# Bulk loads beside the steps of an attention kernel: two parts of 512 KB in a step instead of three of 256 KB

## The chip, the cores and the metric

The kernel runs on one core of one Trainium2 chip. Its time is the device time of one execution in microseconds (us), as the median of several runs; less is better. A profile of one execution gives the rows that are quoted here. In it PE is TensorE, DVE is VectorE, ACT is ScalarE, POOL is GpSimd and SP is SyncE, which does nothing here but issue transfers. A name with q (ACTq, SPq) is the engine's instruction queue while it issues a transfer.

## The reference

Four layers follow one another on `x` of 4 images x 512 channels x 32x32, all in float32, each as x + layer(group_norm(x)). The change touches only the first, an attention over T = 1024 tokens whose 8 heads are mixed before the softmax:

```python
q = einsum('oc,bct->bot', w_q, xf).reshape(b, heads, hd, t)     # k and v likewise
attn = einsum('bhdq,bhdT->bhqT', q, k) * hd ** -0.5
attn = einsum('gh,bhqT->bgqT', w_head, attn)                    # the head mix
attn = softmax(attn, axis=-1)
attn = (attn - mean) / sqrt(var + EPS) * in_gamma + in_beta     # mean, var over queries and keys of a head
out  = einsum('bhqT,bhdT->bhqd', attn, v)
out  = out.reshape(b, t, c) @ w_proj.T + b_proj                 # then back to channels, added to x
```

Behind it come a gate per channel from a small simulated quantum circuit (layer 1), an ordinary attention of 8 heads (layer 2) and a lookup of the 8 best rows out of 2048 in a memory (layer 3).

## The kernel before

Layer 0 takes the images one after another, and each image in 32 steps of 32 query rows. What is made of an image in its steps runs on for some steps into those of the next one, so that the projections of the last image and the preparation of the next lie beside the steps of the present one.

A step, in the order in which the engines get its work:

- PE makes the scores of the first half of the keys into the PSUM tile `sc` (L423), and ACT copies them to `ss` (L429).
- Then comes whatever was planned for the beginning of the step; the bulk loads are there. They are issued on ACT's queue by `beside` (L249).
- PE mixes the heads of an earlier step (`mix`, L443) from the tile `s2`, ACT takes the exponential of the two halves (`exps`, L450), DVE turns the result (`turn_keys`, L456).
- PE makes the scores of the other half of the keys, and ACT copies them to `ss` as well.
- Eight transfers of 128 KB from `ss` to `s2`, the relay (L436, `s<-ss` in the profile), bring the 8 heads of a query together on the partitions, as the mix needs them. Four are issued by SP and four by POOL, in turn.

The relay of step s is read by the mix of two steps later. `ss` and `s2` have two buffers each, so the first copy to `ss` in step s + 2 also waits for the relay of step s to have read it. Each engine keeps the order in which its work is written (`pin`).

Besides, SP issues stores of pieces (`o<-o` L562, `x<-xr` L626), and POOL transfers for the row sums (L515, L523).

The bulk loads are two generators, advanced once in a step, and each advance issues the next group:

- `next_image(b, ...)`: the next image `xn` (2 MB) and the weight `w_q` (1 MB; after the last image the operand of layer 2, `Wq`), in steps 28 to 31 of each image.
- `collect(b, last)`: the attention's output `of` of the image before (2 MB, back from DRAM) and the projection weight `w_p` (1 MB), in steps 7 to 10 of images 1 to 3. The last image's is loaded in another way (`last`), which the change doesn't touch.

Both use `in_threes`: a list of twelve loads of 256 KB, 128 rows of 2 KB each, three in a step over four steps. Steps 28 and 29 load six parts of `xn`, step 30 the last two and a part of `w_q`, step 31 the three others; in `collect` likewise, where the tile for `w_p` is taken in step 9.

After the steps, the weight is used by `take_q` and by `put_quarter`, and `xn` is normalised in place (L357) as the image's statistics are there.

Of the kernel before, what the change touches and what calls it, by code (L numbers as in the profile page):

```python
# [19 lines left out]
T = 1024  # L20
KC = C // P
TC = T // P
NB = 512
# [18 lines left out]
def fast_net(ctx: ExitStack, tc: tile.TileContext, a: dict, out: bass.AP, flag: bass.AP):  # L42
# [43 lines left out]
    for i in range(P // NH):  # L86
        nc.scalar.dma_start(
            out=whp[i * NH:(i + 1) * NH], in_=a["w_head"].rearrange("r m g -> (r m) g")
# [13 lines left out]
        out=gavg_v, in_=gavg_v, compare_op=ALU.is_ge, fill=0.0, base=0,  # L102
# [3 lines left out]
        out=gavg_v, in_=gavg_v, compare_op=ALU.is_ge, fill=0.0, base=GSZ - 1,  # L106
# [99 lines left out]
    o_rows = [dram.tile([P, TC, NB], F32, tag=f"o_{b}", name=f"o_{b}") for b in range(B)]  # L206
# [22 lines left out]
    def big(tag, name):  # L229

        return apool.tile([P, KC, T], F32, tag=tag, name=name)
# [3 lines left out]
    def eight_k(shape, name, at=None):  # L235

        if at is None:
            at = turns8[0] % 3
            turns8[0] += 1
        return apool.tile(shape, F32, tag=f"w{at}", name=name)  # L240
# [6 lines left out]
    def beside(out, in_):  # L247

        pin(nc.scalar.dma_start(out=out, in_=in_))  # L249

    def in_threes(loads):

        for i in range(0, len(loads), 3):
            for out, in_ in loads[i:i + 3]:
                beside(out, in_)
            yield

    def next_image(b, key, src):

        I = img[b]  # L260
        xn = I["xn"] = big("xn", f"xn_{key}{b}")
        w = I[key] = eight_k([P, KC, C], f"{key}_{b}", 2)
        return in_threes([
            (xn[:, k, n * NB:(n + 1) * NB], src[:, k, n * NB:(n + 1) * NB])
            for k in range(KC) for n in range(T // NB)
        ] + [(w[:, k], a[key][:, k]) for k in range(KC)])

    def run_out(gen):
        for _ in gen:
# [296 lines left out]
    def collect(b, last):  # L566


        I = img[b]
        if last:  # L570
            I["of"] = o_full
            nc.sync.dma_start(out=wp_full, in_=a["w_proj"])
            nc.sync.dma_start(out=I["of"].rearrange("p (j x) -> p j x", j=TC), in_=o_rows[b])
            return
        I["of"] = big("xn", f"of_{b}").rearrange("p k t -> p (k t)")
        of = I["of"].rearrange("p (j x) -> p j x", j=TC)
        yield from in_threes([(of[:, j], o_rows[b][:, j]) for j in range(6)])
        w = I["w_p"] = eight_k([P, KC, C], f"w_p_{b}", 2)
        yield from in_threes([(of[:, j], o_rows[b][:, j]) for j in range(6, TC)] + [
            (w[:, k], a["w_proj"][:, k]) for k in range(KC)])  # L580

    def instance_norm(b):

# [589 lines left out]
    def early(b, s):  # L1173

        if b > 0 and s == TC - 1:
            state["load"] = collect(b - 1, False)
        if s == NEXT:
            state["load"] = (
                next_image(0, "Wq", x1[0]) if b + 1 == B else next_image(b + 1, "w_q", x_v[b + 1]))
        next(state["load"], None)  # L1180
# [28 lines left out]
    for b in range(B):  # L1209
# [19 lines left out]
        if last:  # L1229
            run_out(collect(b, True))  # L1230
# [70 lines left out]
    for s in range(len(tiles) + 3):  # L1301
        if s < len(tiles):
            b, tt = tiles[s]
# [664 lines left out]
@with_exitstack  # L1968
def net_kernel(ctx: ExitStack, tc: tile.TileContext, a: dict, out: bass.AP):


    with tc.tile_pool(name="keep", bufs=1) as keep:
        flag = keep.tile([1, 1], mybir.dt.int32, tag="flag", name="flag")
        fast_net(tc, a, out, flag)
        again = tc.nc.values_load(flag, min_val=0, max_val=1)
    with tc.If(again > 0):
        general_net(tc, a, out)
# [61 lines left out]
```

## Time and profile before

| what | value |
|---|---|
| time before, median of 4 runs | 2789.9 us (2782.71 to 2797.22) |
| the profiled execution | 2787.62 us, of which 2785.9 us are its span |
| mean granted TensorE clock of the profiled execution | 0.978 |
| PE busy | 2612.4 us, 94% of the span |
| ACT, DVE, POOL busy | 36%, 55%, 45% |
| mean rate of the DMA engines | 126 GB/s |
| loads that the change touches | `of<-o` 24, `xn_w_q<-in_x` 24, `w_q<-in_w_q` 12, `w_p<-in_w_proj` 12, `xn_Wq<-x` 8 and four of `Wq`, 256 KB each |

All times in the profile are microseconds from the start of the span. The page gives busy times of each engine, the chain of work that ended last, followed back from the end, and groups of instructions: the line and the engine, what was written and read, how often, then the busy time and the mean duration in ns, then the idle time ahead of it and what ended most of that. The granted clock is the share of TensorE's full speed that the chip allowed; at 0.50 a matmul takes twice as long. Layer 0 lies before some 1290 us of the span; the first steps of the four images start at 82.9, 376.4, 694.7 and 1015.4 us, and step 28 of image 1 at 585.8 us.

### The profile page before, as it was taken

The page shows a single profiled execution, that of the slowest core. Times are in us where ns is not written, and L with a number is a line of the kernel's source. Part 1 is how long each engine was busy: PE and PEld are TensorE (multiplying, and loading weights), DVE is VectorE, ACT ScalarE, POOL GpSimd, SP SyncE. Part 2 cuts the span into 40 slices and gives each one's busy share as a digit, 9 for nine tenths or more (in the row PEclk, how much of TensorE's full clock was granted, in tenths as well). Part 3 has the DMA queues.
Part 4 walks back from the last instruction along what each step waited for, and adds up shares of the span by engine and source line. Part 5 has one row for each costly group of instructions (what it writes and reads, how often), then busy time and mean ns, then how long its engine had stood idle before and what let it go on. Part 6 is the DMA issues. An engine that isn't in the chain of part 4 may idle for free.

```text
span 2785.9 us, 46740 instructions
## 1 busy us (share of the span) xinstructions
PE 2612.4 (94%) x18158; PEld 1166.7 (42%) x18158; DVE 1530.9 (55%) x2403; ACT 1002.4 (36%) x1128; POOL 1257.8 (45%) x1959
## 2 busy tenths in 40 slices
PE   7988998989989898989999999999999999999994
PEld 3443444545445444545433433343343334444442
DVE  4487336872578526873245234423623446888886
ACT  0465336551565326551154024214502532221210
POOL 2276415652455515563076026305602635666664
PEclk9999999999999999999999999999999999999997
DMA  2487437880688627785300030021002016766664
GB/s 76 108 209 205 130 85 208 215 222 36 155 220 206 162 77 191 197 212 183 128 17 1 30 121 1 16 82 54 1 30 91 1 35 191 215 187 215 185 183 144
DMA packets 159704, 349.83 MB, mean 126 GB/s; under 512 B 32745, under 2 KB 65513, under 8 KB 155762
## 3 DMA queue, kind: packets, MB, share of 16 engines
q1 hardware_dynamic: 86304, 167.04, 20.9%
q0 software_dynamic: 51584, 142.95, 18.9%
q10 hardware_dynamic: 21586, 36.76, 4.5%
q8 instruction: 146, 2.39, 0.3%
q14 instruction: 84, 0.69, 0.1%
HBM read 178.59 MB, written 33.69 MB: 76 GB/s over the span
## 4 chain that ended last, share of the span: by engine, by line
PE 74%; DMA 8%; DVE 5%; ACT 4%; POOL 4%; issue 3%; SPq 1%; ACTq 0%; POOLq 0%; DVEq 0%
PE at L1055 14%; PE mx L183 7%; PE sc L423 6%; PE pv_c L969 6%; PE sc_c L937 5%; DMA s<-ss 5%; PE pv L483 5%; PE pt L385 4%; PE sc L183 4%; PE p L183 3%; PE mx L443 3%; PE v L195 3%; PE k L183 3%; PE q L183 3%; PE pt L656 3%
## 5 line engine op out<-in xcount | busy, mean ns | idle before, releaser
L456 DVE STREAM_TRANSPOSE eT<-e 128x1024 f32<-128x1024 f32 x256 | 317.3, 1242 | 284.7 <-ACT e L450 283.0
L436 POOL DMA_DIRECT2D s<-ss x512 | 259.4, 515 | 380.2 <-ACT ss L429 311.8
L945 ACT ACTIVATE eT<-sc_c 128x1024 f32<-128x1024 f32 x256 | 248.2, 1021 | 361.3 <-PE sc_c L937 359.3
L1072 POOL DMA_INDIRECT got<-in_mem,ix x256 | 279.9, 1093 | 209.6 <-issue 117.1
L429 ACT COPY ss<-sc 128x1024 f32<-128x1024 f32 x256 | 258.9, 1011 | 278.6 <-PE sc L423 202.3
L472 DVE BATCH_NORM_STATS2 st<-e 128x6 f32<-128x256 f32 x1024 | 341.6, 406 | 0.0
L423 PE MATMUL sc<-k,q 64*32 64x512 f32 x4096 | 286.8, 615 | 19.2 <-ACT ss L429 14.6
L953 POOL TENSOR_TENSOR e<-eT 128x1024 f32<-128x1024 f32 x96 | 232.2, 2421 | 149.9 <-ACT eT L945 139.7
L450 ACT ACTIVATE e<-mx 128x1024 f32<-128x1024 f32 x256 | 262.4, 1029 | 60.9 <-PE mx L443 36.8
L954 DVE TENSOR_TENSOR eT<-eT,e 128x1024 f32<-128x1024 f32 x96 | 143.5, 1494 | 235.6 <-POOL e L953 235.4
L483 PE MATMUL pv<-eT,v 128*64 128x128 f32 x4096 | 258.4, 281 | 0.0
L937 PE MATMUL sc_c<-q,k 64*128 64x512 f32 x1024 | 256.0, 619 | 2.3 <-DVE xr L622 2.3
L483 PEld LDWEIGHTS pv<-eT,v 128*64 128x64 f32 x4096 | 228.0, 140 | 66.5 <-issue 65.0
L969 PE MATMUL pv_c<-eT,v 128*64 128x512 f32 x1024 | 249.9, 609 | 2.4 <-ACT eT L945 2.4
L443 PE MATMUL mx<-s,wmix 32*32 32x512 f32 x4096 | 161.1, 628 | 65.2 <-DMA s<-ss 57.4
L1096 DVE SCALAR_TENSOR_TENSOR acc<-got,et,acc 128x512 f32<-128x512 f32 x224 | 168.5, 752 | 8.4 <-DMA got<-in_mem,ix 0.5
L994 DVE RECIPROCAL ri_c<-ri_c 128x512 f32<-128x512 f32 x32 | 107.2, 3351 | 113.1 <-ACT ri_c L993 113.1
L937 PEld LDWEIGHTS sc_c<-q,k 64*128 64x128 f32 x1024 | 89.0, 187 | 152.3 <-issue 130.0
L950 POOL TENSOR_TENSOR eT<-eT 128x1024 f32<-128x1024 f32 x32 | 78.8, 2463 | 147.5 <-ACT eT L945 147.5
L998 POOL DMA_DIRECT2D fcw<-ri_c x64 | 33.2, 519 | 245.1 <-DVE ri_c L994 245.0
L559 POOL TENSOR_TENSOR o<-pv,rb 64x256 f32<-64x256 f32 x128 | 111.2, 869 | 72.2 <-ACT pv L546 65.3
L1060 ACT COPY att<-at 128x1024 f32<-128x1024 f32 x64 | 64.8, 1012 | 218.6 <-PE at L1055 218.5
(313 smaller groups left out, 3332.3 us busy)
## 6 DMA issues: line engine op xcount, KB each, us to landing
s<-ss SPq DMA_DIRECT2D x512, 128.0 KB
s<-ss POOLq DMA_DIRECT2D x512, 128.0 KB
rb<-r POOLq DMA_DIRECT2D x64, 128.0 KB
o<-o SPq DMA_DIRECT2D x32, 256.0 KB
xr<-in_x ACTq DMA_DIRECT2D x32, 256.0 KB
x<-xr SPq DMA_DIRECT2D x32, 256.0 KB
xr_c<-x SPq DMA_DIRECT2D x32, 256.0 KB
x<-xr_c SPq DMA_DIRECT2D x32, 256.0 KB
```

The costliest lines, as they stand in the source:

```text
L183: pin(nc.tensor.matmul(ps[:, n, :], w[:, k, m * P:(m + 1) * P], rhs(k, n), start=(k == 0), stop=(k == KC - 1),))
L423: pin(nc.tensor.matmul(sc[m * NS:(m + 1) * NS, r, :], q[r * HD:(r + 1) * HD, m, s * NS:(s + 1) * NS], k_[r * HD:(r + 1) * HD, m, n * NB:(n ...
L429: pin(nc.scalar.copy(ss[:, :, n * NB:(n + 1) * NB], sc))
L436: pin(relays[r].dma_start(out=s2[r * KC + m::NH], in_=ss[m * NS:(m + 1) * NS, r, :]))
L450: pin(nc.scalar.activation(e[:, half].rearrange("p r qq k -> p (r qq k)"), flat2(pairs[f"mx{half}"]), AF.Exp))
L456: pin(nc.vector.transpose(eT[:, j % 2].rearrange("p b (qq i r) x -> p i r qq b x", qq=2, i=4)[:, i, 2 * half:2 * half + 2], e[:, half].rea ...
L472: pin(nc.vector.bn_stats(st[:, i, 2 * half + r, qq, :], e[:, half, r, qq, :]))
L483: pin(nc.tensor.matmul(pv[r * HD:(r + 1) * HD, gp, :], I["v"][:, t, g * HD:(g + 1) * HD], eT[:, j % 2, t, :, 4 * g:4 * g + 4], start=(t == ...
L937: pin(nc.tensor.matmul(sc[:, r, :], I["k"][r * HD:(r + 1) * HD, m, t * P:(t + 1) * P], I["q"][r * HD:(r + 1) * HD, m, n * NB:(n + 1) * NB] ...
L969: pin(nc.tensor.matmul(pv[r * HD:(r + 1) * HD, :], I["v"][:, t, h * HD:(h + 1) * HD], e[:, r, :], start=(t == 0), stop=(t == TC - 1),))
L1055: pin(nc.tensor.matmul(sc[:, n * NB:(n + 1) * NB], xn3[b][:, k, tt * P:(tt + 1) * P], memT[k][:, i0:i0 + NB], start=(k == 0), stop=(k == K ...
L1072: pin(nc.gpsimd.indirect_dma_start(out=got[:, i, :], out_offset=None, in_=a["mem"], in_offset=bass.IndirectOffsetOnAxis(ap=ix[:, i:i + 1], ...
```

## The change

The loads are cut into parts twice as large: `xn` into four parts of 512 KB, one for each k with all its tokens in a row of 4 KB, `of` into four parts of two row blocks each, and each weight into two halves of 512 KB with rows of 4 KB (`halves_of`). `in_pairs` issues two in a step. The twelve loads of a stream become six and its four steps three: 28, 29 and 30, and in `collect` 7, 8 and 9. The tile of `w_p` is taken in step 9, as before. Steps 31 and 10 issue none of them any more.

```diff
-    def in_threes(loads):
-        for i in range(0, len(loads), 3):
-            for out, in_ in loads[i:i + 3]:
+    def in_pairs(loads):
+        for i in range(0, len(loads), 2):
+            for out, in_ in loads[i:i + 2]:
                 beside(out, in_)
             yield
 
+    def halves_of(w, key):
+        return [(w[:, k:k + 2], a[key][:, k:k + 2]) for k in (0, 2)]
+
     def next_image(b, key, src):
...
-        return in_threes([
-            (xn[:, k, n * NB:(n + 1) * NB], src[:, k, n * NB:(n + 1) * NB])
-            for k in range(KC) for n in range(T // NB)
-        ] + [(w[:, k], a[key][:, k]) for k in range(KC)])
+        return in_pairs([(xn[:, k], src[:, k]) for k in range(KC)] + halves_of(w, key))
...
     def collect(b, last):
...
-        yield from in_threes([(of[:, j], o_rows[b][:, j]) for j in range(6)])
+        yield from in_pairs([
+            (of[:, j:j + 2], o_rows[b][:, j:j + 2]) for j in range(0, TC, 2)])
         w = I["w_p"] = eight_k([P, KC, C], f"w_p_{b}", 2)
-        yield from in_threes([(of[:, j], o_rows[b][:, j]) for j in range(6, TC)] + [
-            (w[:, k], a["w_proj"][:, k]) for k in range(KC)])
+        yield from in_pairs(halves_of(w, "w_proj"))
```

On PE, DVE and POOL the instructions stand in the same order as before. ACT has 42 fewer issues. Behind line 266 the changed file's lines have numbers higher by one.

## The prediction

> **What bounds the kernel now.** I read the page first, then the waits, then the stretches around the loads by window, then the chain and the order of issue inside one of them. The profiled execution took 2787.62 us, of which 2785.9 us is its span; the four plain runs have a median of 2789.9 us, 2.3 us above it. I work out a difference within the profiled execution and add it to the median.
>
> The page, its chain and two rows of its groups:
>
> ```profile
> PE 74%; DMA 8%; DVE 5%; ACT 4%; POOL 4%; issue 3%; SPq 1%; ACTq 0%; POOLq 0%; DVEq 0%
> ...
> L429 ACT COPY ss<-sc 128x1024 f32<-128x1024 f32 x256 | 258.9, 1011 | 278.6 <-PE sc L423 202.3
> ...
> L443 PE MATMUL mx<-s,wmix 32*32 32x512 f32 x4096 | 161.1, 628 | 65.2 <-DMA s<-ss 57.4
> ```
>
> TensorE carries 74% of the chain, and ACT's queue, which issues the loads that change, none of it. The place where the loads can matter is the last row: the head mix L443 waits 57.4 us in all for the relay `s<-ss`, the eight 128 KB transfers of each step. A usual step takes 7.0 to 7.4 us and has no such wait. The stretches of image 1 by window (columns: length, then busy time and count for PE, PEld, DVE, ACT, POOL, then clock, DMA share, GB/s) are its steps 28, 29, 30, 31, and then step 29 of images 2 and 3:
>
> ```profile
> 585.80:592.50 6.70, 5.41 (x104) 2.52 (x80) 4.85 (x11) 3.86 (x5) 3.77 (x11) 1.00 0.91 240
> 592.50:603.80 11.30, 5.16 (x96) 2.33 (x96) 7.49 (x18) 4.35 (x6) 5.64 (x15) 0.94 0.94 221
> 603.80:614.10 10.30, 9.71 (x116) 5.23 (x131) 5.60 (x12) 5.05 (x6) 5.74 (x14) 0.57 0.92 240
> 614.10:622.10 8.00, 7.96 (x147) 4.43 (x128) 4.56 (x9) 7.21 (x8) 5.57 (x10) 1.00 0.73 211
> ```
> ```profile
> 913.50:924.70 11.20, 5.17 (x96) 2.34 (x97) 8.22 (x19) 4.37 (x6) 5.71 (x16) 0.94 0.95 230
> 1230.10:1241.50 11.40, 5.11 (x96) 2.21 (x79) 8.30 (x19) 4.35 (x5) 6.71 (x18) 0.82 0.98 242
> ```
>
> Step 29 has 5.2 us of PE work in 11.3 us while the DMA engines are 94% busy: it is bound by the transfers. Step 30 has PE at 9.71 of 10.30, at a granted clock of 0.57: bound by a slow TensorE. The same shape is in `collect`: step 9 takes 11.6, 13.9 and 11.6 us in images 1 to 3. That makes six long stalls; image 0's `next_image` has two shorter gaps (4.25 us at 276.98 and 3.89 us at 299.60). PE over that stall, and the chain through it:
>
> ```profile
> 596.74 1.09 PE L423 MATMUL sc<-k,q 64*32 64x512 f32 x16 [0.18 <-ACT ss L429]
> 603.93 2.02 PE L443 MATMUL mx<-s,wmix 32*32 32x512 f32 x32 [6.10 <-DMA s<-ss]
> 605.88 2.00 PE L423 MATMUL sc<-k,q 64*32 64x512 f32 x16
> ```
> ```profile
> 586.12 0.51 ACTq L249
> ...
> 586.67 9.13 DMA xn_w_q<-in_x
> ...
> 595.82 0.54 SPq L436
> ...
> 596.39 2.12 SPq L436
> ...
> 599.43 4.30 DMA s<-ss
> 603.73 0.20 issue
> 603.93 2.02 PE mx L443 x32
> ```
>
> The mix of step 28 waits 6.10 us, then runs 2.02 us where it took 1.20 before. In the chain a load of step 28 takes 9.13 us to land, an SP relay goes out the moment it has (595.82), and the relays' end releases PE.
>
> **The order in the transfers.** By landing times in the trace, transfers finish in the order of issue, whichever queue they are in. An SP relay issued at 594.64, alone on its queue, landed at 602.36; the load that ACT had issued ahead of it, at 593.71, landed at 602.56, and POOL's relays issued at 592.36 and 592.86 at 599.31 and 599.79. So the price of a load is what it adds ahead of the relay that comes last. *Trainium skill, "DMA: Bandwidth & Descriptors", section "Queues, rings and completion order", says the opposite: each engine takes turns between the queues, a packet at a time. By that rule the lone SP relay would have passed the loads, bigger loads would cost the relays next to nothing, and the sum below would lose its first term and end near -4 us.* I go by the trace.
>
> **The change, part by part.**
>
> *Same bytes, fewer issues.* Seven load streams of 3 MB (21 MB) go out in 42 issues instead of 84. An issue on ACT is 0.33 to 0.51 us when the queue is short and up to 1.4 us when it is deep; three in step 28 took 2.31 us (585.76), and the first exp started after them (588.19). With two, that exp can start some 0.5 to 1.2 us earlier in steps 28, 29, 7 and 8. Nothing follows from it: in steps 28 and 29 PE then waits for the relay anyway. In step 31, which loses all its issues (1.67 us at 614.11), PE is busy 7.96 of 8.00 us; in step 10 the exp waits for a mix at the half clock. I put all of these at 0; if that cover failed, step 31 would give 0.8 us back in each of three images.
>
> *Rows of 4 KB.* Uncontended packets take 84 ns for 2 KB and 159 ns for 4 KB: 5% less for the same bytes. Three 256 KB loads alone landed 0.64 us apart (459.82, 460.46, 461.10), which is about 400 GB/s. Of a stream, 8 parts lie ahead of the critical relay: 8 x 0.64 x 5% = 0.26 us, x6 stalls = -1.5 us. *The same page, section "Measured", has the rule to batch into 1 MiB or more for 75% of peak; it speaks for the change, but no row here shows the 256 KB parts as slow, and the 5% is all that I count.*
>
> *More bytes ahead of the critical relay.* This is the main term. Before, the relay of step 28 comes after six parts (steps 28 and 29), 1.5 MB; after, behind four of 512 KB, 2 MB. The relay of step 8 likewise has steps 7 to 9 ahead of it: by then 2.25 MB with the first of `w_p`, later 2.5 to 3 MB, of which the part of step 7 drains in free time (DMA share 0.72 at 429 to 438), so again about 512 KB more. An extra 256 KB costs 0.64 us if it moves as three loads alone do, and 1.1 us at the mixed rate of these stretches (240 x 6.7 + 221 x 11.3 = 4105 KB in 18.0 us, 228 GB/s). The extra parts lie in the mixed stretch, so I take 1.1: 2.2 us a stall. Against it, the DMA engines were idle 0.09 x 6.7 + 0.06 x 11.3 = 1.3 us there, partly since SP held relays back; I give 0.5 us of that to the new order. So 1.7 us a stall, x6 = +10 us. Ends: 0 (0.64 x 2, all idle time used) and 2.2 x 6 = +13.
>
> *Waits of SP.* SP's and ACT's transfers share eight semaphores in turn, and a transfer waits for the landing of the eighth before it. Before, the second and third SP relays of step 28 wait for loads 1 and 2 (issued 594.64 and 595.82 instead of about 590.7 and 591.3); after, only the fourth waits, for the second 512 KB load, which by order of landing is there at about 596.5. Queued behind it on SP are the store `x<-xr` and the relays of step 29, which start at 598.6 to 599.4 now: about the same. So three of four relays go out 4 to 5 us earlier, the fourth as before. As landing goes by issue, the last one sets the mix: 0, with a gain of up to one relay, 0.6 us, a stall. ACT's fourth load now waits for the first of step 28 to land (about 594.6), so ACT's exp of step 29 starts 0.3 us later, under the stall: 0. PE's, DVE's and POOL's orders are unchanged.
>
> *Steps 10 and 31 without loads.* The relays of step 30 no longer share with `w` loads. In images 1 to 3 PE is busy there: 0. In image 0 the mix at 299.60 waits 3.89 us behind three of them: 2 us of gap go, and with a gap near 2 us the half clock of 298.68 to 305.51 may not come (gaps of 2.1 to 2.8 us mostly left the clock at 1.00, those from 3.9 us on halved it). That is worth up to 3.4 us; I take half: -3.7 us together, +0.9 for one more part ahead of the mix at 276.98: -2.8.
>
> Sum: +10 - 1.5 - 2.8 = about +5.5 us: 2793.1 for a profiled execution, **2795.4** against the median. With the ends (0 to +13; -5.5 to +0.9 in image 0; -1.5; -2.4 in step 31; -3.6 for the SP waits) the sum runs from -13 to +14, and its likely part from -6 to +14: 2784 to 2804.
>
> **The rivals.**
>
> *A second stall (slower).* Place: the mix one step later, at 613.92 and at the start of step 11 (463.0). It has no wait now; the relays of step 29 landed by 610.43, 3.5 us early, those of step 9 by 459.41, 3.6 us early. Step 30 now starts with 1 MB instead of 768 KB, and in `collect` the last SP relay of step 9 waits for the first half of `w_p`, which lands at about 455 where that relay now goes out at 449.58. If they land over 3.5 us later, six mixes wait again, and a gap of 3 us can bring another half clock (3.1 us in step 30: 10.3 against 7.2). Price: six times 2 to 4 on top of the sum: +15 to +30, 2805 to 2820. For it: the DMA share of 0.92 in step 30. Against it: `w` is not ahead of POOL's relays of step 29, which are issued earlier.
>
> *The early relays win (faster).* If the fourth relay alone doesn't hold the mix for long, the relays end with POOL's, which landed at 599.79, 3.7 us before the last of SP. The gap of 6.10 falls to about 2.4 us and the half clock after it may go: 3.7 + 3.1 = 6.8 us in three images, and part of it in `collect`: -15 to -25, 2765 to 2775. For it: SP waited 5.4 us for loads in step 28 to 30. Against it: DMA shares of 0.94 to 0.98, so that earlier issue finds no free engine.
>
> *It does nothing.* The order of landing may hide both: within 2 us of before.
>
> **How the numbers follow.** A measurement of this kernel tells 0.5% (14 us) from no change: below 2776 is faster, above 2804 slower. The sum gets 0.55, of which 0.12 above 2804, as every term can be a little over; the second stall 0.25; the early relays 0.17; nothing 0.03. So faster 0.17, same 0.43 + 0.03 = 0.46, slower 0.12 + 0.25 = 0.37. The range, 2774 to 2815, leaves out most of the early relays' case (0.14) and the top of the second stall's (0.06).
>
> **What would show it.** Right: step 29 of images 1 to 3 and step 9 at 13 us instead of 11.3, with the wait PE `mx` <- DMA `s<-ss` up by some 10 us from 57.4; step 31 unchanged at 8.0; the gap at 299.6 down to 2 us. The first relay after a 512 KB load landing behind it would confirm the order of issue. Wrong: step 29 at 9 us or less with a clock of 1.00 in step 30 (early relays), or a new wait at the mix of step 31 or 11 (second stall). If all stalls stay at their lengths, the extra bytes were hidden in idle DMA time.

## The result and the profile after

The changed kernel takes 1.0026 times the time before (95% interval 1.0019 to 1.0034). On the median of 2791.13 us that the kernel before has over all its runs, this is +7.3 us (+5.3 to +9.5). The forecast was +5.5 us, inside the 0.5% that count as no change, and the time lies in its range. The profiled execution took 2793.21 us, 2791.5 us of it its span; the one before took 2787.62 us.

The page after, the lines that answer to the first fence of the prediction (lines of the file are higher by one):

```profile
PE 74%; DMA 10%; ACT 5%; DVE 4%; POOL 4%; issue 2%; SPq 1%; ACTq 0%; POOLq 0%; DVEq 0%
...
L430 ACT COPY ss<-sc 128x1024 f32<-128x1024 f32 x256 | 259.0, 1012 | 306.2 <-PE sc L424 196.2
...
L444 PE MATMUL mx<-s,wmix 32*32 32x512 f32 x4096 | 159.5, 627 | 77.6 <-DMA s<-ss 73.1
```

The transfers have 10% of the chain instead of 8%, and the mix waits 73.1 us for the relays instead of 57.4: some 16 us more. The forecast had said some 10 us more. PE's own work at L444 is the same (159.5 and 161.1 us), and the mean granted clock is 0.980 instead of 0.978, so the loss does not come from the half clock. Not all of the 16 us reach the time. Up to the last mix of layer 0, PE is busy 3.9 us less (1151.4 us instead of 1155.3), and a wait of 3.9 us in image 0, which the profile before puts down to ACT and not to the relays, is gone. So the last mix ends 8.3 us later, at 1279.1 us instead of 1270.8.

Where it is, by window. The columns are the stretch, its length, busy time and count for PE, PEld, DVE, ACT and POOL, then clock, DMA share and GB/s. First steps 28 to 30 of image 1 after the change, and step 29 of images 2 and 3:

```profile
589.05:597.38 8.33, 5.41 (x98) 2.52 (x80) 7.25 (x18) 3.97 (x4) 5.59 (x16) 1.00 0.97 252
597.38:608.62 11.24, 6.75 (x96) 3.37 (x96) 5.08 (x10) 4.57 (x6) 4.06 (x10) 0.85 0.90 226
608.62:616.63 8.01, 7.50 (x116) 3.25 (x131) 3.93 (x8) 5.10 (x5) 3.66 (x8) 0.79 0.95 270
...
919.11:931.10 11.99, 5.10 (x96) 2.34 (x96) 7.08 (x17) 4.47 (x6) 6.11 (x16) 0.81 1.02 270
1242.30:1254.39 12.09, 5.12 (x96) 2.37 (x96) 6.57 (x15) 4.35 (x6) 5.64 (x15) 0.85 1.03 266
```

Step 29 is 0.7 to 0.8 us longer in images 2 and 3. In image 1 it is as long as before (11.24), and step 28 took the time instead: 8.33 us where it had 6.70. Step 30 of image 1 gave that back in this execution: 8.01 us at a clock of 0.79, where it had 10.30 at 0.57. So in this pair of profiles steps 28 to 30 together are shorter in images 1 and 3 (27.6 and 27.0 us instead of 28.4 and 27.6) and longer in image 2 alone (28.7 instead of 27.2); more profiles are compared further down. Now step 9 of images 1 to 3, before and then after:

```profile
443.40:455.04 11.64, 5.06 (x96) 2.24 (x79) 8.20 (x19) 4.35 (x6) 7.84 (x18) 0.88 1.02 240
762.02:775.93 13.91, 5.11 (x96) 2.23 (x79) 8.53 (x19) 4.35 (x5) 9.08 (x22) 0.78 0.93 219
1082.38:1093.96 11.58, 5.13 (x100) 2.26 (x83) 8.36 (x19) 4.34 (x6) 7.90 (x18) 0.85 1.03 247
```
```profile
445.34:458.01 12.67, 5.03 (x96) 2.23 (x78) 7.87 (x19) 4.34 (x5) 7.76 (x18) 0.90 0.98 263
763.79:779.27 15.48, 5.03 (x96) 2.22 (x78) 7.87 (x19) 4.34 (x5) 9.58 (x22) 0.79 0.94 227
1088.98:1104.68 15.70, 5.05 (x100) 2.26 (x82) 7.87 (x19) 4.34 (x5) 8.94 (x21) 0.76 0.95 217
```

The same 5.0 to 5.1 us of PE work, in 1.0, 1.6 and 4.1 us more. So in these profiles `collect` lost more than `next_image`, against the forecast's 1.7 us for each of the six. The chain shows what ends the longest of them, in image 3 after the change (columns: start, length, what):

```profile
1087.58 0.69 POOL vsum L406
1088.26 1.22 POOL rb L524 x2
...
1090.71 1.53 POOL s L437 x3
1092.24 12.22 DMA s<-ss
1104.46 0.20 issue
1104.66 1.88 PE mx L444 x17
```

The critical relay, the one that lands last, is POOL's last of step 8. POOL issued it at 1092.24, and it took 12.22 us to land. POOL had been kept by two small transfers, as its timeline shows (columns: start, length, then in brackets the idle time ahead and what ended it), before and after:

```profile
1079.16 1.41 POOL L405 DMA_DIRECT2D vsum<-vs  x2 [3.47 <-DMA vs<-vrow]
...
1083.01 2.03 POOL L436 DMA_DIRECT2D s<-ss  x4 [0.42 <-issue]
```
```profile
1086.84 1.42 POOL L406 DMA_DIRECT2D vsum<-vs  x2 [4.55 <-DMA vs<-vrow]
...
1090.71 2.04 POOL L437 DMA_DIRECT2D s<-ss  x4 [0.42 <-issue]
```

POOL waits for the store `vs<-vrow` to land (3.47 us before, 4.55 us after, with more load bytes in front), then issues `vsum<-vs` and `rb<-r`, and only then the four relays of step 8. ACT's issues at the start of step 9, before and then after:

```profile
1082.38 0.87 ACTq L249 DMA_DIRECT2D of<-o  x2
1083.29 0.44 ACTq L249 DMA_DIRECT2D w_p<-in_w_proj  x1
```
```profile
1088.99 0.84 ACTq L249 DMA_DIRECT2D w_p<-in_w_proj  x2
```

Step 9 starts at 1088.98 after the change, and ACT issues both halves of `w_p` there at once (1088.99 to 1089.83). So a whole MB of `w_p` stands ahead of the relays. Before, step 9 started at 1082.38, its loads were 768 KB, and POOL's first relay left at 1083.01, ahead of the issue of the third load (1083.29).

### The profile page after: what moved, and what is told of

Its sections match the earlier page's. It is cut to its first block, busy times and chain, and to the rows that moved or that the text cites. A ratio compares the mean times of both kernels' runs of the same rounds, so it can differ in the third digit from the quotient of the medians.

```text
span 2791.5 us, 46697 instructions
## 1 busy us (share of the span) xinstructions
PE 2604.1 (93%) x18158; PEld 1162.2 (42%) x18158; DVE 1529.5 (55%) x2403; ACT 1004.1 (36%) x1128; POOL 1259.5 (45%) x1959
## 3 DMA queue, kind: packets, MB, share of 16 engines
q1 hardware_dynamic: 86304, 167.04, 20.7%
## 4 chain that ended last, share of the span: by engine, by line
PE 74%; DMA 10%; ACT 5%; DVE 4%; POOL 4%; issue 2%; SPq 1%; ACTq 0%; POOLq 0%; DVEq 0%
PE at L1056 15%; PE mx L183 7%; PE sc L424 7%; DMA s<-ss 6%; PE pv_c L970 6%; PE sc_c L938 6%; PE pv L484 5%; PE pt L386 4%; PE sc L183 4%; PE p L183 4%; ACT ss L430 3%; PE v L195 3%; PE k L183 3%; PE q L183 3%; PE pt L657 3%
## 5 line engine op out<-in xcount | busy, mean ns | idle before, releaser
L430 ACT COPY ss<-sc 128x1024 f32<-128x1024 f32 x256 | 259.0, 1012 | 306.2 <-PE sc L424 196.2
L424 PE MATMUL sc<-k,q 64*32 64x512 f32 x4096 | 288.5, 619 | 17.8 <-ACT ss L430 13.2
L444 PE MATMUL mx<-s,wmix 32*32 32x512 f32 x4096 | 159.5, 627 | 77.6 <-DMA s<-ss 73.1
```

What stands on the lines that cost most here:

```text
L424: pin(nc.tensor.matmul(sc[m * NS:(m + 1) * NS, r, :], q[r * HD:(r + 1) * HD, m, s * NS:(s + 1) * NS], k_[r * HD:(r + 1) * HD, m, n * NB:(n ...
L430: pin(nc.scalar.copy(ss[:, :, n * NB:(n + 1) * NB], sc))
```

## The experiments

The theories: A, the bytes that a step puts ahead of the critical relay set the loss; B, the size of a part does, as an SP relay waits for a whole part; C, rows of 4 KB hurt the relays; D, POOL's late relays in `collect` are what makes the loads cost. Ratios are to the kernel before, with 95% intervals. A step starts when ACT begins to copy the first half of its scores (L429, L430 after the change). The table gives for `collect`, from one profiled execution each and as means over images 1 to 3: when step 10 starts and when POOL issues its last relay of step 8 (both counted from the start of step 7), and how long that relay takes to land.

| kernel | step 10 starts, us | last relay issued, us | it lands after, us | ratio |
|---|---|---|---|---|
| before | 26.4 | 16.5 | 9.6 | 1 |
| next_only (collect as before) | 24.9 | 15.8 | 8.8 | 1.0003 (0.9990 to 1.0016) |
| changed | 28.5 | 17.0 | 11.3 | 1.0026 (1.0019 to 1.0034) |
| collect_only | 29.0 | 17.1 | 11.6 | 1.0033 (1.0020 to 1.0047) |
| rows_2k | 28.5 | 17.1 | 11.1 | 1.0037 (1.0019 to 1.0054) |
| fours_256 | 27.4 | 16.8 | 10.2 | 1.0031 (1.0015 to 1.0047) |
| mixed_768 | 27.2 | 16.6 | 10.4 | 1.0000 (0.9985 to 1.0015) |
| wp_later | 25.4 | 16.5 | 8.6 | 1.0011 (0.9996 to 1.0026) |
| half_wp | 24.9 | 16.5 | 8.1 | 1.0027 (1.0012 to 1.0043) |
| pairs_wp_later | 23.2 | 16.6 | 6.3 | 0.9991 (0.9979 to 1.0004) |
| vsum_late | 24.1 | 14.5 | 7.3 | 0.9988 (0.9973 to 1.0003) |
| after_vsum_late | 24.0 | 13.8 | 7.9 | 0.9978 (0.9963 to 0.9994) |
| pairs_wp_vsum_later | 22.3 | 13.8 | 7.8 | 0.9950 (0.9933 to 0.9967) |
| best | 20.9 | 14.0 | 5.8 | 0.9943 (0.9929 to 0.9958) |

**Small parts, 1 MB a step (fours_256).**

```diff
-        return in_pairs([(xn[:, k], src[:, k]) for k in range(KC)] + halves_of(w, key))
+        return in_groups([(xn[:, k, n * NB:(n + 1) * NB], src[:, k, n * NB:(n + 1) * NB])
+            for k in range(KC) for n in range(T // NB)
+        ] + [(w[:, k], a[key][:, k]) for k in range(KC)], (4, 4, 4))   # collect likewise
```

> Parts of 256 KB with rows of 2 KB as before, but four in a step over three steps, so 1 MB a step as in the changed kernel. Theory A (the bytes a step puts ahead of the critical relay): the stalls of the changed kernel come back though the parts are small: +5 to +10 us over before, long steps 9 and 29 about 1 to 4 us longer than before. Theory B (the size of a part: a relay that waits for a 512 KB part to land waits longer): as before, within 2 us, since no part is larger. Theory C (rows of 4 KB disturb the relays): as before too.

Measured: 1.0031, +8.7 us. The loss is there with parts of 256 KB and rows of 2 KB, which is against B and C. Its place differs somewhat: step 10 starts 1.8 us later than the mean of the two kernels with the old `collect`, and steps 28 to 30 together are 29.3 us in images 1 to 3, where the five profiled kernels with three 256 KB parts a step have 27.2 us.

**Large parts, 768 KB a step (mixed_768).**

```diff
+        return in_pairs([
+            (xn[:, 0], src[:, 0]), (xn[:, 1, 0:NB], src[:, 1, 0:NB]),
+            (xn[:, 1, NB:T], src[:, 1, NB:T]), (xn[:, 2], src[:, 2]),
+            (xn[:, 3], src[:, 3]), (w[:, 0], a[key][:, 0]),
+            (w[:, 1], a[key][:, 1]), (w[:, 2:4], a[key][:, 2:4])])   # collect likewise
```

> One part of 512 KB (rows of 4 KB) and one of 256 KB in a step, over four steps: 768 KB a step as before, eight parts instead of twelve. Theory A (bytes a step): as before, -2 to +3 us. Theory B (size of a part) and theory C (rows of 4 KB): two thirds of the bytes are in large parts with long rows, so two thirds of the change, +4 to +6 us.

Measured: 1.0000 (-4 to +4 us), as A says; the upper end touches the lower end of B and C. With the run before it, the bytes a step and not the size of a part carry the loss; an effect of the size below some 4 us would not show here.

**The two halves of the change.** next_only has the new `next_image` and the old `collect`, collect_only the reverse.

```diff
-        return in_pairs([(xn[:, k], src[:, k]) for k in range(KC)] + halves_of(w, key))
+        return in_threes([...])      # collect_only; next_only keeps in_threes in collect instead
```

> The change in next_image alone (steps 28 to 30 of four images), collect as before. From the gaps of PE ahead of the mix in the two profiles (+1.9 -0.2 in image 0, +1.2, +1.7, +0.8 and -2.7 at the end) about +2.6 us; from the sum of the prediction +1.4 us. If instead the early relays pay here, -3 us or less.

Measured: 1.0003, +0.8 us (-2.8 to +4.5).

> The change in collect alone (steps 7 to 9 of images 1 to 3), next_image as before. From the gaps in the two profiles (+1.1, +1.9, +4.3) about +7 us; from the sum of the prediction (three stalls of 1.7 us less the rows) +4.3 us. If the two parts of the change are independent, this and next_image alone add up to the whole, +7 us.

Measured: 1.0033, +9.2 us (+5.6 to +13.1). Within the intervals, the loss of the change is all that of `collect`. The two sum to +10 us where the whole has +7.3, which the intervals allow.

**`w_p` later.** wp_later starts from the kernel before, pairs_wp_later and half_wp from the changed one.

```diff
+        yield from in_groups([(of[:, j], o_rows[b][:, j]) for j in range(TC)], (3, 3, 2))
+        w = I["w_p"] = eight_k([P, KC, C], f"w_p_{b}", 2)
+        yield from in_groups([(w[:, k], a["w_proj"][:, k]) for k in range(KC)], (2, 2))   # wp_later
...
+            (of[:, j:j + 2], o_rows[b][:, j:j + 2]) for j in range(0, TC, 2)], (2, 2, 0))
+        yield from in_groups(halves_of(w, "w_proj"), (1, 1))   # pairs_wp_later; half_wp has (2, 2) above
```

> The kernel before, but the four 256 KB parts of w_p go out two in step 10 and two in step 11 (before: one in step 9 and three in step 10). So 256 KB less stand ahead of POOL's last relays of step 8, which end the stall of step 9. Theory A (bytes ahead of the critical relay): 0.65 to 1.1 us less in each of three stalls, -2 to -3.5 us against before. Theory D (POOL issues those relays late, and the bytes do not matter): no change.

Measured: 1.0011 (-1 to +7 us): no gain, A's figure of -2 to -3.5 us did not come. Step 10 starts about as early as with the old `collect` (25.4 us against 26.4 and 24.9), and from there to step 12 it takes 15.1 us instead of the 14.1 of the kernel before: the moved parts cost there what they saved.

> The changed kernel, but the two 512 KB halves of w_p go out one in step 10 and one in step 11 instead of both in step 9: 1 MB less ahead of POOL's last relays of step 8. Theory A: the stall of step 9 falls by 2.6 to 4.4 us in three images, so the whole loss of the change goes, 0 to -6 us against before. Theory D: as the changed kernel, +5 to +9 us against before.

Measured: 0.9991 (-6 to +1 us): the loss is gone, as A says, with 512 KB parts of `of` still in pairs. D in the form of this expectation, that the bytes do not matter, falls. Step 10 starts at 23.2 us. POOL issues its last relay at 16.6 us, no earlier, and it lands after 6.3 us.

> The changed kernel, but of the two 512 KB halves of w_p one goes out in step 9 and one in step 10, so 512 KB instead of 1 MB of w_p can stand ahead of POOL's relays of step 8. A dose between two kernels that have run: 1 MB ahead gave +7.3 us (the changed kernel), none gave -2.5 us (w_p in steps 10 and 11). If the bytes ahead of POOL's late relays set the stall, the time lies between, +0 to +5 us against before, and step 10 starts 24 to 27 us after step 7 instead of 26.6 to 29.6. If it is the place of of's 512 KB parts in steps 7 and 8 that costs, +5 to +9 us.

The relay's time to land follows the dose: 6.3 us with no `w_p` in step 9, 8.1 us with 512 KB, 11.3 and 11.6 us with 1 MB. That is about 1.3 us for 256 KB over the whole MB. The timed runs do not follow: 1.0027 (+3 to +12 us), although step 10 starts at 24.9 us. The dose is thus shown for the landing of the relay, and not for the time of the kernel. In half_wp's one profile steps 7 to 11 of images 1 to 3 are 4.1 us shorter than before; what is longer there is image 0's steps 7 to 27, by 6.4 us, which its edit does not touch. Where half_wp loses what the timed runs show stays open.

**POOL's small transfers later (vsum_late, after_vsum_late).**

```diff
         nc.gpsimd.dma_start(out=vs_row[b], in_=row)
-        vsum = I["vsum"] = small.tile(...)      # and its two transfers
+    def bring_v(b): ...                         # these
...
         if s == TC - 1:
             sum_v(b)
+        if s == 18:
+            bring_v(b)
```

> The kernel before, but POOL's two transfers vsum<-vs (4-byte elements) move from step 7 to step 18. POOL no longer waits there for vs<-vrow to land (from 6.7 to 10.3 us after the start of step 7) ahead of its four relays of step 8, which it issued at 14.5 to 17.6 us. Theory D (POOL's late issue and the slow small transfers set the stall): the relays go out 2 to 4 us earlier and the stall of step 9 falls by 2 to 4 us in three images, with the half clock after it in some: -6 to -18 us. Theory A alone (bytes): the small transfers carry next to no bytes, 0 to -2 us.

These two transfers are not held in program order, and in the built kernel POOL issues them right behind its four relays of step 8, not in step 18. That serves the question: the relays no longer wait for `vs<-vrow`. Measured: 0.9988 (-8 to +1 us), less than the -6 to -18 us that D named. POOL's last relay goes out 2 us earlier, at 14.5 us. But the step gains less: SP's last relay of step 8 now lands last, at 22.6, 23.9 and 25.3 us after the start of step 7 in images 1 to 3, and step 10 starts at 22.8, 24.0 and 25.5.

> The changed kernel with the same move of vsum<-vs to step 18. Theory D, in which the change's cost in collect comes from large loads beside the small transfers: no loss is left, within 2 us of the kernel before with the same move. Theory A: the loss stays, 4 to 10 us above the kernel before with the same move, as 512 KB more stand ahead of the relays either way.

Measured: 0.9978 (-10 to -2 us), no slower than vsum_late, whose interval it overlaps. No loss of the change is left, which is D and against A as far as it says "either way". POOL's timeline in image 3 of after_vsum_late says why; its step 9 starts at 1083.81, and ACT issues the halves of `w_p` from 1083.82 on:

```profile
1082.19 2.03 POOL L440 DMA_DIRECT2D s<-ss  x4 [3.00 <-DMA s<-ss]
...
1084.56 0.75 POOL L409 DMA_DIRECT2D vsum<-vs  x1
```

The relays are ahead of the 1 MB. In the changed kernel the first of them leaves 1.7 us after the start of step 9, with the 1 MB already issued.

**Rows of 2 KB in parts of 512 KB (rows_2k).**

```diff
-        return [(w[:, k:k + 2], a[key][:, k:k + 2]) for k in (0, 2)]
+        return [(w[:, k::2], a[key][:, k::2]) for k in (0, 1)]
...
+            (xn[:, k:k + 2, n * NB:(n + 1) * NB], src[:, k:k + 2, n * NB:(n + 1) * NB])
+            for k in (0, 2) for n in range(T // NB)      # and of[:, j::4]
```

> The changed kernel's parts of 512 KB, two in a step in the same steps, but each cut from two pieces with rows of 2 KB instead of rows of 4 KB. If the row width is worth its 5% of packet time, 0.26 us a stall and some 1.5 us in all more than the changed kernel: +7 to +11 us against before. If rows of 4 KB were what hurts the relays (theory C), 0 to +3 us against before.

Measured: 1.0037 (+5 to +15 us), and step 10 starts as in the changed kernel. C falls. Whether the wide rows save the 1.5 us of the sum can't be read from two intervals that overlap.

**Put together (best, pairs_wp_vsum_later).** In both, `of` goes out in pairs of 512 KB in steps 7 and 8, the halves of `w_p` one each in steps 10 and 11, and `vsum<-vs` as in vsum_late. They differ in `next_image`: three parts of 256 KB a step in best, two of 512 KB in the other.

> A version put together from what paid: in collect of in 512 KB parts, two in steps 7 and 8, the halves of w_p one each in steps 10 and 11; POOL's vsum<-vs in step 18; next_image in 256 KB parts, three in a step, as before. If the gains of collect add up, -6 to -14 us against before; the long step 9 of images 1 to 3 then ends 20 to 23 us after the start of step 7 instead of 24 to 30. If SP's last relay, which waits for a load, now sets the end alone, -3 to -6 us.

Measured: 0.9943 (0.9929 to 0.9958), -16 us: faster than both kernels. It gains more than the two edits did apart. The landings say why: the mix waits for POOL's and for SP's last relay of step 8, which before land 26.1 and 24.2 us after the start of step 7. pairs_wp_later brings them to 22.9 and 20.8 us, vsum_late to 21.8 and 23.9, and best to 19.9 and 20.7, so that either edit alone leaves one of the two behind. Step 9 of images 1 to 3 by window:

```profile
441.94:449.36 7.42, 5.03 (x96) 2.20 (x77) 6.87 (x17) 4.34 (x5) 6.55 (x15) 1.00 0.96 225
755.63:761.82 6.19, 5.11 (x96) 2.21 (x78) 5.64 (x11) 4.35 (x6) 5.42 (x14) 1.00 0.86 223
1073.85:1081.39 7.54, 5.03 (x96) 2.20 (x77) 6.99 (x17) 4.34 (x5) 6.69 (x15) 1.00 1.01 236
```

It is a step of usual length again, and the wait of the mix for the relays is 46.7 us over the whole execution.

> The same as the version put together from what paid, but with next_image in 512 KB parts, two in a step, as in the changed kernel. The difference between the two is the price of next_image's part of the change with collect undisturbed: 0 to +5 us by the profiles of both kinds (steps 28 to 30 about 1.4 us longer in images 1 to 3), 0 if it gives all of it back in step 31.

Measured: 0.9950 (0.9933 to 0.9967), 0.0007 above best, which is 2 us and inside the intervals: the price of `next_image`'s part is small, as next_only says.

## Why the prediction was right, and where its steps were not

*The direction and the main term.* More bytes ahead of the critical relay make it land later: shown for the time by the pair fours_256 and mixed_768 and by pairs_wp_later, and for the landing by the dose of `w_p`, which half_wp's time does not follow. The rate taken, 1.1 us for 256 KB, fits `collect`: for the 512 KB more that the prediction counts, the last relay takes 2.3 us longer to land; over the whole MB of `w_p` the dose gives 1.3. By the rule of the Trainium skill that the prediction weighed ("DMA: Bandwidth & Descriptors", section "Queues, rings and completion order"), engines take turns between the queues; the prediction took from it that bigger loads would cost the relays next to nothing. The relay's 6.3, 8.1 and 11.3 us decide against that price. They do not rule out turns as such, and the order of landing is not strictly the order of issue either, as the fourth relay shows below.

*The same price for all six stalls.* This is the term that was mis-sized. In `collect` step 10 starts at 28.5 and 29.0 us with the new loads and at 26.4 and 24.9 us with the old ones: 3.1 us a stall instead of 1.7. It has two parts. The last relay takes 11.3 to 11.6 us to land instead of 8.8 to 9.6, so 2.3 us more; the sum had 2.2 for it and took off 0.5 for idle DMA time, which does not show here. And POOL issues it 0.9 us later, as the small store `vs<-vrow` for which POOL waits lands 0.8 us later, 11.3 us after the start of step 7 instead of 10.4 (means of two profiles each). That second wait was no part of the sum: it counted the relays behind the loads, but not what POOL waits for ahead of its relays. after_vsum_late shows that the two depend on POOL's order: with the relays ahead of `w_p` nothing is lost.

*The stalls of `next_image`.* Over the profiled kernels of either kind (five with 256 KB in threes, six with 512 KB in pairs) steps 28 to 30 take 0.9, 1.0 and 2.0 us more in images 1 to 3, 1.3 us on average. 1.7 was near. The sign that the prediction named, a step 29 of 13 us, did not come: it has 11.2, 12.0 and 12.1 us. Step 9 has 12.7 to 15.7.

*The fourth SP relay "as before".* Here the step was wrong by some 3 us in image 1. The relay should have gone out at about 596.5, that is 10.7 us into step 28. The chain of image 1 after the change:

```profile
589.42 13.45 DMA xn_w_q<-in_x
602.87 0.02 issue
602.89 5.55 DMA s<-ss
608.44 0.24 issue
608.68 1.79 PE mx L444 x32
```

The second 512 KB load lands 13.8 us into the step, and the relay that waits for it ends the stall. SP's wait for the loads, which the early relays were to shorten, has grown from 5.4 to 11.0 us between 585 and 616 us. About half of the 3 us did not reach PE, as this relay then landed in 5.55 us where its like took 7.1 before: step 30 starts 19.6 us into step 28 and started 18.0 us into it before, 1.6 us later. In images 2 and 3 the fourth relay went out 10.9 and 11.9 us into step 28 (before 10.9 and 10.1), so nearly as the prediction said.

The prediction named a sign for its order of issue, that the first relay after a 512 KB load lands behind it. The trace does not show it for this load: it was issued at 589.42 and landed at 602.87, while the first relay after it, SP's of 592.35, landed at 601.37. Each transfer raises its semaphore sixteen times in the trace. Of this load fifteen of the sixteen had come by 599.99, and the last came 2.9 us later. The order of issue thus holds roughly: 10 of the 36 loads of the changed kernel landed after a transfer that was issued later, by up to 4.4 us, and 13 of the 72 before the change.

*Image 0.* The gain of 2.8 us did not come. PE's rows at these mixes, before and then after:

```profile
299.60 2.02 PE L443 MATMUL mx<-s,wmix 32*32 32x512 f32 x32 [3.89 <-ACT xn_w_q L357]
```
```profile
281.21 2.02 PE L444 MATMUL mx<-s,wmix 32*32 32x512 f32 x32 [6.12 <-DMA s<-ss]
298.42 2.02 PE L444 MATMUL mx<-s,wmix 32*32 32x512 f32 x32 [3.65 <-DMA s<-ss]
```

The prediction put the gap of 3.89 us down to the relay; the profile puts it down to ACT's normalising (L357), which ended at 299.55, where the relay had landed at 299.46. This gap is gone, but one of 3.65 us stands at the mix ahead of it, at 298.42, and the gap of 4.25 us at the start of step 29 has grown to 6.12. Over the same profiled kernels steps 28 to 30 are 2.8 us longer there, of which the time up to the next image's first step gives 2.2 us back. So +0.6 us, 3.4 us more than forecast, an error the same way as that in `collect`.

*The rest.* ACT's saved issues gave nothing that a run shows: in step 31 of image 1, from 616.63 to 624.20, PE is busy 7.53 of 7.57 us after the change as well (7.96 of 8.00 before). The 1.5 us of the wider rows stays unsettled.

*The rivals.* The second stall came only in image 0, at the start of step 31 (3.65 us), while the gap at the mix behind it is gone. At the start of step 11 there is none: step 10 of image 1 takes 8.0 us after as before. The early relays did not win: in images 1 to 3 SP's first three relays of step 28 land by 15.0 us into it, but the fourth lands at 17.8 to 19.4, and the mix waits for it. So the forecast of +5.5 us came out near +7.3 us with its first term right in kind. Its split was off: `collect` +4.3 us (three times 1.7, less the rows) where collect_only shows +9.2 (+5.6 to +13.1), and `next_image` +1.4 us where next_only shows +0.8. That the sum is within 2 us of the measurement is in part luck, with `collect` taken at less than half of what it showed alone.

*Left open.* The profiles' own differences add up to more than the timed runs show, 9.9 us over steps 7 to 11 of images 1 to 3 (means of two profiles each) and some 4 us in `next_image` against +7.3 us in all. Steps 12 to 27 of image 0 alone vary by 8 us between profiles of kernels that do the same there, so single profiles can't settle a few us.

## What to carry to other kernels

Where transfers land roughly in the order of issue, as here, a load's price is paid by the latest small transfer that is issued behind it, and by whoever that transfer holds. So look first for who issues late, and why: moving POOL's two small transfers behind its relays, and the loads out of the step in which those relays go, was worth more (-16 us) than any size of part. A step's share of the bytes matters, the size of a part hardly.

## What the runs showed of the hardware

Two edits that gave some 3 us each (pairs_wp_later, vsum_late; neither clear of zero by itself) gave 16 us together: two relays on different queues end the same wait, and in vsum_late SP's still landed last where POOL's had been brought forward. And a 512 KB load among the relays landed 13.45 us after its issue, where 256 KB loads alone land 0.64 us apart: in such a stretch what is issued around it sets the time to landing more than its size. Last, a transfer lands with the slowest of its sixteen increments: over the 36 loads of the changed kernel the last came 0.47 us (median) and up to 2.88 us after the one before it, so a relay that waits for one load can be held by a small share of it.
